# One stage of a four-layer kernel re-ordered by hand: taps of a depthwise convolution moved from VectorE to TensorE, projection and transposes shifted against it

## The chip, the core and the metric

The kernel runs on one core of a Trainium2 chip. TensorE (PE) multiplies matrices and writes to PSUM, VectorE (DVE) and ScalarE (ACT) work elementwise, GpSimd (POOL) copies and multiplies, and SyncE (SP) issues most transfers. The metric is the device time of one execution in microseconds; the median of the runs is given. All data is fp32.

## The reference

The input is x, 8 images of 64 x 64 positions with 192 channels. Four layers each add something to x after a group norm. Layer 0 is a state-space block with convolutions and a feed-forward part, layers 2 and 3 are depthwise 3x3 convolutions. Layer 1 is a scan in four directions; the change lies in its first part:

```
x   = group_norm(x)
xz  = einsum('bhwc,oc->bhwo', x, in_proj_w)         # 192 -> 768 channels
xa, z = split(xz, 2)                                # 384 + 384
u   = silu(depthwise_conv3x3(xa) + conv_b)          # 'SAME', one 3x3 filter a channel
xs  = u, u transposed in space, and both reversed   # the 4 directions
x_dbl = einsum('bkdl,kcd->bkcl', xs, x_proj_weight) # 44 values a position and direction
...                                                 # then the scan over 4096 positions
```

## The kernel before

The program is a sequence of stages: layer 0 (`layer0`), the input stage of layer 1 (`layer1_in`), its scan (`layer1_scan`), and a tail that ends layer 1 and does layers 2 and 3. Each stage reads the last one's result from device memory.

The input stage works on 64 strips: 8 images of 8 strips, a strip being 8 image rows of 64 positions, 512 columns. Channels lie on partitions; the 384 inner channels are three tiles of 128. One strip goes through this:

- `normed` (L690 to L697): load the strip of x1 (`xt`, 384 KB, by SP), and scale and shift it on ACT (`g`, L695, two instructions).
- `project` (L750): for each of three channel tiles two matmuls over the 192 input channels into a PSUM bank "mm"; ACT copies the bank into `xa` (L754), a buffer of ten rows: the strip's eight and one of each neighbour. POOL copies the neighbouring rows between this strip's buffer and the last one's (L758, L759) or clears them at an image's edge (L736, L738).
- `convolve`: for each tile the three taps of the middle column (1, 4, 7 of 0 to 8, with tap = 3 dy + dx + 1) run on PE as matmuls with diagonal matrices (L774) into a bank "cv"; ACT adds the bias and writes `u` (L776); DVE adds the other six taps, each one instruction of 504 elements a partition (L784: 63 of 64 columns, as the outermost has no neighbour).
- `finish` (L797): one Silu on ACT over all three tiles of `u`. It is written into the order after the first tile's bias of the next strip.
- `turn`: SP stores `u` (`ur`, L807). For each of four blocks of 128 positions PE transposes three tiles into a bank "tp" (L813) and multiplies by `w_xp` into a bank "xp" (L816); ACT copies the one into `uT` (L820), DVE the other into `xdt` (L821). SP stores both (`ut` L822, `xd` L823).

All pools of PSUM banks have two buffers. The order of the instructions on PE, DVE, ACT and POOL is that of the program text (`every_engine`, a manual schedule); SP's queue takes its transfers in order too. The text is produced by `together`, which runs the three generators `turn`, `convolve` and `project` in turn, one stretch up to the next `yield` each, while `done` holds back a generator that is too far ahead. So the strip that is turned is the one before the strip that is convolved, and the projection is one to two strips ahead.

Of the kernel before, what the change touches and what calls it, by code (L numbers as in the profile page):

```python
# [10 lines left out]
AF = mybir.ActivationFunctionType  # L11
ALU = mybir.AluOpType
# [3 lines left out]
B, H, W, C = 8, 64, 64, 192  # L16
L = H * W
CP, CT = 96, 2
DIN = 384
DP, DT = 128, 3  # L20
NH, HD, NS = 6, 64, 64
N1, R1, K1 = 16, 12, 4
XC = R1 + 2 * N1
DFF = 768
EPS = 1e-5
NJ = 512
NCH = L // NJ


class Names:  # L30
    n = 0


def mk(pool, shape, tag, **kw):
    Names.n += 1
    return pool.tile(shape, F32, tag=tag, name=f"{tag}_{Names.n}", **kw)


def make_diag(nc, pool, w, nct, ident, tag, plus_one=False):
    P = w.shape[0]  # L40
    dg = mk(pool, [P, nct, 3, P], tag)
    for ct in range(nct):
        for j in range(3):
            s = w[:, ct, 3 * j + 1 : 3 * j + 2]
            if j == 1 and plus_one:
                nc.vector.scalar_tensor_tensor(dg[:, ct, j, :], ident[:P, :P], s, ident[:P, :P], ALU.mult, ALU.add)
            else:
                nc.vector.tensor_scalar(dg[:, ct, j, :], ident[:P, :P], s, None, ALU.mult)
    return dg


# [22 lines left out]
def together(*threads, beside=()):  # L74

    threads = list(threads)
    while threads:
        for t in list(threads) + list(beside):
            if next(t, threads) is threads and t in threads:
                threads.remove(t)  # L80


def every_engine(tc):
    ET = mybir.EngineType
    return tc.manual_schedule(engines={ET.PE, ET.DVE, ET.Activation, ET.Pool})
# [586 lines left out]
def layers123(ctx: ExitStack, tc, a, dr, x1, mv1, out, cst):  # L672
# [30 lines left out]
    xd = [mk(dr, [L, K1, 1 + XC], f"xd{b}") for b in range(B)]  # L703
    yk = [[mk(dr, [L, DIN], f"y{b}_{k}") for k in range(K1)] for b in range(B)]
    layer1_in(tc, a, load, w_in, normed, ur, ut, xd, cst)
    layer1_scan(tc, a, load, ur, ut, xd, yk, cst)
    x2 = [mk(dr, [CP, CT, L], f"x2d{b}") for b in range(B)]
# [4 lines left out]
@with_exitstack  # L712
def layer1_in(ctx: ExitStack, tc, a, load, w_in, normed, ur, ut, xd, cst):

    nc = tc.nc
    ident = cst[0]
    wp = ctx.enter_context(tc.tile_pool(name="wi1", bufs=1))
    cw, cb = load("conv_w", [DP, DT, 9]), load("conv_b", [DP, DT])
    w_xp = load("w_xp", [DP, DT, K1 * XC])
    dg = make_diag(nc, wp, cw, DT, ident, "dg")  # L720
    sb = ctx.enter_context(tc.tile_pool(name="si1", bufs=2))
    psum = ctx.enter_context(tc.tile_pool(name="pi1", bufs=2, space=PSUM))
    xdt = [mk(wp, [128, NJ // 128, K1, 1 + XC], f"xdt{i}") for i in range(2)]
    for t in xdt:
        nc.vector.memset(t, 1.0)
    R = NJ // W
    strips = [(b, r) for b in range(B) for r in range(NCH)]
    rows, us = {}, {}
    done = {"in": 0, "conv": 0, "out": 0}

    def xa_rows(q):

        if q not in rows:
            t = rows[q] = mk(sb, [DP, DT, (R + 2) * W], "xa", bufs=4)
            if strips[q][1] == 0:
                nc.gpsimd.memset(t[:, :, 0:W], 0.0)  # L736
            if strips[q][1] == NCH - 1:
                nc.gpsimd.memset(t[:, :, (R + 1) * W :], 0.0)  # L738
        return rows[q]

    def project():
        _, g = normed(sb, *strips[0])
        for q, (b, r) in enumerate(strips):
            while done["conv"] < q - 2:
                yield
            t = xa_rows(q)
            for o in range(DT):
                ps = mk(psum, [128, NJ], "mm")
                for ct in range(CT):
                    nc.tensor.matmul(  # L750
                        ps, w_in[:, ct, o * 128 : (o + 1) * 128], g[:, ct, :], start=ct == 0, stop=ct == CT - 1
                    )
                yield
                nc.scalar.copy(t[:, o, W : W + NJ], ps)  # L754
            if q + 1 < len(strips):
                _, g = normed(sb, *strips[q + 1])
            if r > 0:
                nc.gpsimd.tensor_copy(t[:, :, 0:W], rows[q - 1][:, :, NJ : NJ + W])  # L758
                nc.gpsimd.tensor_copy(rows[q - 1][:, :, NJ + W :], t[:, :, W : 2 * W])  # L759
            done["in"] = q + 1  # L760
            yield

    def convolve():
        for q, (b, r) in enumerate(strips):
            while done["in"] < q + 1 + (r < NCH - 1) or done["out"] < q - 2:
                yield
            t = rows[q]
            u = us[q] = mk(sb, [DP, DT, NJ], "u", bufs=4)
            uv = u.rearrange("p d (h w) -> p d h w", w=W)
            tv = t.rearrange("p d (h w) -> p d h w", w=W)  # L770
            for o in range(DT):
                ps = mk(psum, [128, NJ], "cv")
                for dy in range(3):
                    nc.tensor.matmul(ps, dg[:, o, dy, :], t[:, o, dy * W : dy * W + NJ], start=dy == 0, stop=dy == 2)  # L774
                yield
                nc.scalar.activation(u[:, o, :], ps, AF.Identity, bias=cb[:, o : o + 1])  # L776
                if o == 0 and q > 0:
                    finish(q - 1)
                yield
                for dy in range(3):  # L780
                    for dx in (-1, 1):
                        w0, w1 = max(0, -dx), W - max(0, dx)
                        tap = 3 * dy + dx + 1
                        nc.vector.scalar_tensor_tensor(  # L784
                            uv[:, o, :, w0:w1],
                            tv[:, o, dy : dy + R, w0 + dx : w1 + dx],
                            cw[:, o, tap : tap + 1],
                            uv[:, o, :, w0:w1],
                            ALU.mult,
                            ALU.add,  # L790
                        )
            yield
        finish(len(strips) - 1)
        yield

    def finish(q):
        nc.scalar.activation(us[q], us[q], AF.Silu)  # L797
        del rows[q]
        done["conv"] = q + 1

    def turn():
        for q, (b, r) in enumerate(strips):
            while done["conv"] < q + 1:
                yield
            u = us.pop(q)
            t0 = r * NJ
            nc.sync.dma_start(ur[b][:, :, t0 : t0 + NJ], u)  # L807
            uT = mk(sb, [128, NJ // 128, DIN], "uT")
            xt = xdt[q % 2]
            for i in range(NJ // 128):  # L810
                ps = mk(psum, [128, NJ], "tp")
                for o in range(DT):
                    nc.tensor.transpose(ps[:, o * 128 : (o + 1) * 128], u[:, o, i * 128 : (i + 1) * 128], ident)  # L813
                px = mk(psum, [128, NJ], "xp")
                for o in range(DT):
                    nc.tensor.matmul(  # L816
                        px[:, 0 : K1 * XC], u[:, o, i * 128 : (i + 1) * 128], w_xp[:, o, :], start=o == 0, stop=o == 2
                    )
                yield
                nc.scalar.copy(uT[:, i, :], ps[:, 0:DIN])  # L820
                nc.vector.tensor_copy(xt[:, i, :, 1:], px[:, 0 : K1 * XC].rearrange("p (k c) -> p k c", k=K1))  # L821
            nc.sync.dma_start(ut[b][t0 : t0 + NJ, :].rearrange("(t q) d -> q t d", q=128), uT)  # L822
            nc.sync.dma_start(xd[b][t0 : t0 + NJ].rearrange("(t q) k c -> q t k c", q=128), xt)  # L823
            done["out"] = q + 1
            yield

    with every_engine(tc):
        together(turn(), convolve(), project())


@with_exitstack
# [621 lines left out]
```

## Time and profile before

| | |
|---|---|
| median of 3 runs | 25105.1 us (25094.24 to 25116.98) |
| profiled execution, span | 25098.0 us (the page gives no time around it) |
| PE busy over the span | 23784.2 us, 95% |
| DVE | 22334.3 us, 89% |
| ACT | 20190.7 us, 80% |
| POOL | 17651.1 us, 70% |
| input stage, first projection to last copy of `xdt` | 5319.4 to 6654.0 us |
| granted TensorE clock, mean | 0.967 |

The shares over the span are averages over stages: the scan alone takes the time from about 6680 to 23000 us. For a change in the input stage its own stretch has to be read. A matmul's busy time in a group holds its latency, and matmuls overlap, so the distance between starts says more of what one costs than the mean of one. An fp32 matmul of the program stands in the trace as two records, a transpose as one. "Idle before, releaser" tells who ended an engine's wait.

### The profile page before, as it was taken

The numbers are of one execution on the slowest core, as the hardware profiler recorded it, in microseconds if no ns is written. First come the engines' busy times: TensorE is split into PE (matmuls) and PEld (weight loads), VectorE is DVE, ScalarE is ACT, GpSimd is POOL, SyncE is SP. The second block draws the span as 40 slices with busy tenths as digits, with TensorE's granted clock in tenths as the row PEclk, the third lists the DMA queues.
The fourth block names the chain that finished last, engine by engine and source line by source line (L and its number), as shares of the span: only waits on it lengthen the run. The fifth ranks groups of instructions, "written<-read, shape, count | busy, mean of one in ns | idle before, by whom it ended". The sixth has DMA issues, their size and how long they took to land.

```text
span 25098.0 us, 445961 instructions
## 1 busy us (share of the span) xinstructions
PE 23784.2 (95%) x156672; PEld 18458.1 (74%) x156672; DVE 22334.3 (89%) x26682; ACT 20190.7 (80%) x40488; POOL 17651.1 (70%) x18332
## 2 busy tenths in 40 slices
PE   8999999988899999999999999999999999998999
PEld 4444444445688888888888888888888888885333
DVE  6777777766799999999999999999999999998887
ACT  4555555544599999999999999999999999997443
POOL 2322322310399999999999999999999999995110
PEclk8888888899999999999999999999999999999999
DMA  1111111123333333333333333333333333335554
GB/s 59 47 43 46 46 47 43 38 70 114 110 100 95 96 101 95 95 103 95 95 101 97 95 99 98 95 97 100 95 95 104 95 95 102 95 95 157 170 175 122
DMA packets 1506272, 2337.12 MB, mean 93 GB/s; under 512 B 249997, under 2 KB 775949, under 8 KB 1504026
## 3 DMA queue, kind: packets, MB, share of 16 engines
q1 hardware_dynamic: 1496858, 2283.42, 31.5%
q8 instruction: 1236, 20.25, 0.3%
q0 software_dynamic: 7168, 25.17, 0.3%
q14 instruction: 1010, 8.27, 0.1%
HBM read 1847.54 MB, written 460.59 MB: 92 GB/s over the span
## 4 chain that ended last, share of the span: by engine, by line
PE 36%; ACT 31%; DVE 13%; POOL 13%; issue 6%; DMA 0%; POOLq 0%; SPq 0%; DVEq 0%; ACTq 0%
ACT dA L1003 13%; POOL hc L1053 11%; ACT sb L987 7%; PE pd L1009 6%; PE yt L942 5%; DVE h L1044 5%; ACT bd L987 4%; PE cv L1282 4%; PE y L592 3%; PE pd L1011 2%; PE mm L901 2%; PE fc L626 2%; PE y L519 1%; PE cv L774 1%; PE tp L564 1%
## 5 line engine op out<-in xcount | busy, mean ns | idle before, releaser
L1053 POOL TENSOR_TENSOR hc<-h,bc 128x512 f32<-128x512 f32 x12288 | 15431.9, 1289 | 475.6 <-DVE h L1044 341.2
L1044 DVE TENSOR_TENSOR_SCAN h<-dA,st,pd 128x512 f32<-128x512 f32 x10752 | 12949.5, 1262 | 530.1 <-PE pd L1009 374.4
L1003 ACT ACTIVATE dA<-dl,A_logs 128x512 f32<-128x512 f32 x12288 | 8817.1, 718 | 47.0 <-DVE h L1044 39.6
L942 PE MATMUL yt<-sq,hc 128*128 128x128 f32 x49152 | 7489.3, 275 | 200.1 <-POOL hc L1053 93.8
L1009 PE MATMUL pd<-bd,dut 128*128 128x128 f32 x49152 | 6581.4, 277 | 254.4 <-DVE h L1044 232.1
L1009 PEld LDWEIGHTS pd<-bd,dut 128*128 128x128 f32 x49152 | 5968.5, 192 | 609.9 <-PE yt L942 342.9
L942 PEld LDWEIGHTS yt<-sq,hc 128*128 128x128 f32 x49152 | 5669.7, 141 | 644.3 <-POOL hc L1053 624.4
L987 ACT ACTIVATE sb<-dut,xt 128x384 f32<-128x384 f32 x8192 | 4779.5, 609 | 1.1 <-DVE dut L928 1.0
L1011 PE MATMUL pd<-sq,sb 128*128 128x128 f32 x24576 | 3739.5, 275 | 8.5 <-DVE h L1044 0.4
L1011 PEld LDWEIGHTS pd<-sq,sb 128*128 128x128 f32 x24576 | 2823.6, 141 | 479.1 <-DVE dl L915 380.8
L987 ACT ACTIVATE bd<-sq,xt 128x128 f32<-128x128 f32 x8192 | 3026.3, 395 | 0.0
L1044 DVE TENSOR_TENSOR_SCAN h<-dA,pd 128x512 f32<-128x512 f32 x1536 | 1770.8, 1204 | 117.0 <-PE pd L1009 67.2
L1143 POOL TENSOR_TENSOR yin<-yin,yin 128x1536 f32<-128x1536 f32 x64 | 233.9, 3655 | 1635.1 <-DMA yin<-y 892.5
L1282 PE MATMUL cv<-x,dgi 96*96 96x512 f32 (+1 forms) x2560 | 1175.0, 595 | 9.3 <-ACT x L1271 9.1
L481 POOL TENSOR_TENSOR xdt<-xb,dtv 128x384 f32<-128x384 f32 x256 | 217.1, 848 | 1186.6 <-ACT xb L475 1186.6
L234 DVE SCALAR_TENSOR_TENSOR x<-xs,cpe_w,x 96x504 f32<-96x504 f32 (+1 forms) x1024 | 886.6, 866 | 31.8 <-ACT x L222 21.7
L784 DVE SCALAR_TENSOR_TENSOR u<-xa,conv_w,u 128x504 f32<-128x504 f32 x1152 | 850.1, 743 | 50.5 <-ACT u L776 12.5
L1282 PEld LDWEIGHTS cv<-x,dgi 96*96 96x96 f32 x2560 | 413.0, 164 | 638.2 <-issue 604.5
L901 PE MATMUL mm<-xs,w_dt 13*128 13x512 f32 x1536 | 863.0, 641 | 1.8 <-DVE dl L915 1.0
L1055 POOL COPY st<-h 128x3 f32<-128x3 f32 x4096 | 825.0, 201 | 0.0
L1303 DVE SCALAR_TENSOR_TENSOR y<-x,wi,y 96x504 f32<-96x504 f32 x1024 | 796.0, 796 | 17.7
L626 PE MATMUL fc<-ff,fc_w 128*96 128x512 f32 x1536 | 791.0, 621 | 2.7 <-DVE xo L629 2.7
(263 smaller groups left out, 26186.7 us busy)
## 6 DMA issues: line engine op xcount, KB each, us to landing
bc<-bcd SPq DMA_DIRECT2D x4096, 256.0 KB
yin<-y SPq DMA_DIRECT2D x256, 768.0 KB
csb<-csd SPq DMA_DIRECT2D x256, 384.0 KB
dut<-ut SPq DMA_DIRECT2D x128, 768.0 KB
y<-ys SPq DMA_DIRECT2D x128, 768.0 KB
dut<-ut SPq DMA_DIRECT2D x256, 384.0 KB
y<-ys SPq DMA_DIRECT2D x256, 384.0 KB
xt<-x1d SPq DMA_DIRECT2D x128, 384.0 KB
```

The lines of the kernel that those rows point to most:

```text
L234: nc.vector.scalar_tensor_tensor(d[:, :, w0:w1], s[:, dy : dy + R, w0 + dx : w1 + dx], w[:, ct, tap : tap + 1], d[:, :, w0:w1], ALU.mult, ...
L626: nc.tensor.matmul(ps, f2w[:, o, ct * CP : (ct + 1) * CP], ff[:, o, :], start=o == 0, stop=o == 5)
L784: nc.vector.scalar_tensor_tensor(uv[:, o, :, w0:w1], tv[:, o, dy : dy + R, w0 + dx : w1 + dx], cw[:, o, tap : tap + 1], uv[:, o, :, w0:w1] ...
L901: nc.tensor.matmul(ps, w_dt[:, k, o * 128 : (o + 1) * 128], made["xs"][0 : 1 + R1, :], start=True, stop=True)
L942: nc.tensor.matmul(yt[:, t * 128 : (t + 1) * 128], src[:, t * 128 : (t + 1) * 128], mat, is_transpose=mat is ident, start=first and t == 0 ...
L987: nc.scalar.activation(v, src, AF.Copy, scale=m["xt"][:, t, 1 + R1 + n : 2 + R1 + n])
L1003: nc.scalar.activation(dA, ready[s]["dl"][:, o, :], AF.Exp, scale=aneg[:, k, o, n : n + 1])
L1009: nc.tensor.matmul(dst, ready[s]["dut"][:, t, cols], brows[g, t], start=True, stop=True)
L1011: nc.tensor.transpose(dst, brows[g, t][:, cols], ident)
L1044: nc.vector.tensor_tensor_scan(h[:, o, rev], decay.pop(j)[:, rev], turned.pop(j)[:, rev], 0.0 if first else st[:, o, n : n + 1], ALU.mult, ...
L1053: nc.gpsimd.tensor_tensor(hc, h[:, o, :], held[g], ALU.mult)
L1282: nc.tensor.matmul(pv[:, :, w0:w1], dgi[:, ct, j, :], sv[:, dy : dy + R, w0 + dx : w1 + dx], start=j == 0, stop=j == len(TAPS) - 1, skip_g ...
```

## The change

Five of the nine taps (the middle column and the middle row: 1, 4, 7, 3, 5) run on PE, four (the corners) on DVE. The generators are gone; the order is written out. The unit is a slot: one channel tile `o` of the strip `c`. In each slot stand, in this order: the five taps of (c, o) on PE; ACT's copy of the projection tile of the slot before; the copies of the blocks turned in the slot before, with the stores after the last block; the Silu of the tile two slots before, now one instruction a tile; bias on ACT and four taps on DVE for (c, o); the projection tile (c+3, o); one turned block of strip c-2 (two in the slot o = 0); and in slot 0 the load and scaling of strip c+4. The loop runs from c = -3 to n+2, and each function does nothing for a strip that does not exist. The ring of `xa` has five buffers instead of four. Which lines of the generators fall away can be seen above; the diff shows what stands in their place.

```diff
--- before.py
+++ after.py
-def make_diag(nc, pool, w, nct, ident, tag, plus_one=False):
+def make_diag(nc, pool, w, nct, ident, tag, taps):
     P = w.shape[0]
-    dg = mk(pool, [P, nct, 3, P], tag)
+    dg = mk(pool, [P, nct, len(taps), P], tag)
...
+        for j, tap in enumerate(taps):
+            nc.vector.tensor_scalar(dg[:, ct, j, :], ident[:P, :P], w[:, ct, tap : tap + 1], None, ALU.mult)
     return dg
-    dg = make_diag(nc, wp, cw, DT, ident, "dg")
+    ON_PE = (1, 4, 7, 3, 5)
+    dg = make_diag(nc, wp, cw, DT, ident, "dg", ON_PE)
...
+    n = len(strips)
+    gs, rows, us, uts = {}, {}, {}, {}
+    banks, turning = {}, []
+
...
+    def reach(tap):
+        dy, dx = tap // 3, tap % 3 - 1
+        return dy, dx, max(0, -dx), W - max(0, dx)
+
+    def normalise(q):
+        if 0 <= q < n:
+            gs[q] = normed(sb, *strips[q])[1]
+
+    def project(q, o):
+        if not 0 <= q < n:
+            return
+        ps = banks["in", q, o] = mk(psum, [128, NJ], "mm")
+        for ct in range(CT):
+            nc.tensor.matmul(
+                ps, w_in[:, ct, o * 128 : (o + 1) * 128], gs[q][:, ct, :], start=ct == 0, stop=ct == CT - 1
+            )
+
+    def projected(q, o):
+        if not 0 <= q < n:
+            return
+        r = strips[q][1]
+        if o == 0:
+            t = rows[q] = mk(sb, [DP, DT, (R + 2) * W], "xa", bufs=5)
+            if r == 0:
                 nc.gpsimd.memset(t[:, :, 0:W], 0.0)
-            if strips[q][1] == NCH - 1:
+            if r == NCH - 1:
                 nc.gpsimd.memset(t[:, :, (R + 1) * W :], 0.0)
-        return rows[q]
-
-    def project():
-        _, g = normed(sb, *strips[0])
-        for q, (b, r) in enumerate(strips):
-            while done["conv"] < q - 2:
-                yield
-            t = xa_rows(q)
+        t = rows[q]
+        nc.scalar.copy(t[:, o, W : W + NJ], banks.pop(("in", q, o)))
+        if o == DT - 1 and r > 0:
+            nc.gpsimd.tensor_copy(t[:, :, 0:W], rows[q - 1][:, :, NJ : NJ + W])
+            nc.gpsimd.tensor_copy(rows[q - 1][:, :, NJ + W :], t[:, :, W : 2 * W])
+
+    def taps_on_pe(q, o):
+        if not 0 <= q < n:
+            return
+        ps = banks["cv", q, o] = mk(psum, [128, NJ], "cv")
+        for i, tap in enumerate(ON_PE):
+            dy, dx, w0, w1 = reach(tap)
+            nc.tensor.matmul(
+                by_rows(ps)[:, :, w0:w1],
+                dg[:, o, i, :],
+                by_rows(rows[q][:, o, :])[:, dy : dy + R, w0 + dx : w1 + dx],
+                start=i == 0,
+                stop=i == len(ON_PE) - 1,
+                skip_group_check=True,
+            )
+
+    def taps_on_dve(q, o):
+        if not 0 <= q < n:
+            return
+        if o == 0:
+            us[q] = mk(sb, [DP, DT, NJ], "u", bufs=4)
+        u = us[q][:, o, :]
+        nc.scalar.activation(u, banks.pop(("cv", q, o)), AF.Identity, bias=cb[:, o : o + 1])
+        for tap in (0, 2, 6, 8):
+            dy, dx, w0, w1 = reach(tap)
+            nc.vector.scalar_tensor_tensor(
+                by_rows(u)[:, :, w0:w1],
+                by_rows(rows[q][:, o, :])[:, dy : dy + R, w0 + dx : w1 + dx],
+                cw[:, o, tap : tap + 1],
+                by_rows(u)[:, :, w0:w1],
+                ALU.mult,
+                ALU.add,
+            )
+        if o == DT - 1:
+            del rows[q]
+
+    def silu(q, o):
+        if not 0 <= q < n:
+            return
+        nc.scalar.activation(us[q][:, o, :], us[q][:, o, :], AF.Silu)
+        if o == DT - 1:
+            b, r = strips[q]
+            nc.sync.dma_start(ur[b][:, :, r * NJ : (r + 1) * NJ], us[q])
+
+    def turn(q, i):
+        if not 0 <= q < n:
+            return
+        u, cols = us[q], slice(i * 128, (i + 1) * 128)
+        ps, px = mk(psum, [128, NJ], "tp"), mk(psum, [128, NJ], "xp")
+        for o in range(DT):
+            nc.tensor.transpose(ps[:, o * 128 : (o + 1) * 128], u[:, o, cols], ident)
+        for o in range(DT):
+            nc.tensor.matmul(px[:, 0 : K1 * XC], u[:, o, cols], w_xp[:, o, :], start=o == 0, stop=o == DT - 1)
+        turning.append((q, i, ps, px))
+
+    def turned():
+        while turning:
+            q, i, ps, px = turning.pop(0)
+            if i == 0:
+                uts[q] = mk(sb, [128, NB, DIN], "uT")
+            nc.scalar.copy(uts[q][:, i, :], ps[:, 0:DIN])
+            nc.vector.tensor_copy(
+                xdt[q % 2][:, i, :, 1:], px[:, 0 : K1 * XC].rearrange("p (k c) -> p k c", k=K1)
+            )
+            if i == NB - 1:
+                b, r = strips[q]
+                t0 = r * NJ
+                nc.sync.dma_start(ut[b][t0 : t0 + NJ, :].rearrange("(t q) d -> q t d", q=128), uts.pop(q))
+                nc.sync.dma_start(xd[b][t0 : t0 + NJ].rearrange("(t q) k c -> q t k c", q=128), xdt[q % 2])
+                del us[q]
+
+    BLOCKS = ((0, 1), (2,), (3,))
+    with every_engine(tc):
+        normalise(0)
+        last = None
+        for c in range(-3, n + 3):
...
             for o in range(DT):
...
-    with every_engine(tc):
-        together(turn(), convolve(), project())
+                taps_on_pe(c, o)
+                if last is not None:
+                    projected(*last)
+                turned()
+                k = DT * c + o - 2
+                silu(*divmod(k, DT))
+                taps_on_dve(c, o)
+                project(c + 3, o)
+                last = c + 3, o
+                for i in BLOCKS[o]:
+                    turn(c - 2, i)
+                if o == 0:
+                    normalise(c + 4)
+        turned()
```

More of the change, by code (lines that the diff above doesn't have):

```diff
@@ L36, in mk @@
     return pool.tile(shape, F32, tag=tag, name=f"{tag}_{Names.n}", **kw)
-def make_diag(nc, pool, w, nct, ident, tag, plus_one=False):
+def make_diag(nc, pool, w, nct, ident, tag, taps):
     P = w.shape[0]
-    dg = mk(pool, [P, nct, 3, P], tag)
+    dg = mk(pool, [P, nct, len(taps), P], tag)
     for ct in range(nct):
[L43 to L48, printed above, removed]
+        for j, tap in enumerate(taps):
+            nc.vector.tensor_scalar(dg[:, ct, j, :], ident[:P, :P], w[:, ct, tap : tap + 1], None, ALU.mult)
     return dg
@@ L719, in layer1_in @@
     w_xp = load("w_xp", [DP, DT, K1 * XC])
-    dg = make_diag(nc, wp, cw, DT, ident, "dg")
+    ON_PE = (1, 4, 7, 3, 5)
+    dg = make_diag(nc, wp, cw, DT, ident, "dg", ON_PE)
     sb = ctx.enter_context(tc.tile_pool(name="si1", bufs=2))
     psum = ctx.enter_context(tc.tile_pool(name="pi1", bufs=2, space=PSUM))
-    xdt = [mk(wp, [128, NJ // 128, K1, 1 + XC], f"xdt{i}") for i in range(2)]
+    NB = NJ // 128
+    xdt = [mk(wp, [128, NB, K1, 1 + XC], f"xdt{i}") for i in range(2)]
     for t in xdt:
@@ L727, in layer1_in, with by_rows @@
     strips = [(b, r) for b in range(B) for r in range(NCH)]
[L728 to L735, printed above, removed]
+    n = len(strips)
+    gs, rows, us, uts = {}, {}, {}, {}
+    banks, turning = {}, []
+    def by_rows(v):
+        return v.rearrange("p (h w) -> p h w", w=W)
+    def reach(tap):
+        dy, dx = tap // 3, tap % 3 - 1
+        return dy, dx, max(0, -dx), W - max(0, dx)
@@ L736, in xa_rows @@
                 nc.gpsimd.memset(t[:, :, 0:W], 0.0)
-            if strips[q][1] == NCH - 1:
+            if r == NCH - 1:
                 nc.gpsimd.memset(t[:, :, (R + 1) * W :], 0.0)
-        return rows[q]
-    def project():
-        _, g = normed(sb, *strips[0])
-        for q, (b, r) in enumerate(strips):
-            while done["conv"] < q - 2:
-                yield
-            t = xa_rows(q)
-            for o in range(DT):
[L748 to L825, printed above, removed]
```

## The prediction

> **What bounds the kernel now.** I read the page's slices first: around 5300 us POOL goes quiet, PE shows 8, 9, 9 and DVE 7, 9, 9, which is the input stage of layer 1. Then the busy time by stretches inside that stage:
>
> ```profile
> core 0: us, PE busy (x) PEld busy (x) DVE busy (x) ACT busy (x) POOL busy (x), PEclk, DMA share, GB/s
> 5560.00:5720.00 160.00, 141.90 (x520) 82.06 (x519) 111.57 (x172) 64.88 (x104) 7.98 (x16) 0.99 0.33 112
> 5720.00:5880.00 160.00, 141.90 (x517) 81.80 (x516) 111.95 (x173) 63.50 (x102) 7.07 (x15) 0.99 0.34 116
> ```
>
> PE is the fullest engine (141.9 of 160 us), DVE is second (112), ACT far behind (64), the DMA engines a third busy. Next the groups of the stretch 5400 to 6520 us, shapes kept apart (x counts instructions; one fp32 matmul of the program stands there as two records, a transpose as one):
>
> ```profile
> L784 DVE SCALAR_TENSOR_TENSOR u<-xa,conv_w,u 128x504 f32<-128x504 f32 x983 | 725.4, 743 | 32.5 <-DVE u L784 0.5
> L774 PE MATMUL cv<-xa,dg 128*128 128x512 f32 x987 | 452.2, 594 | 0.0
> L750 PE MATMUL mm<-g,w_in 96*128 96x512 f32 x656 | 308.6, 592 | 0.0
> L813 PE MATMUL tp<-sq,u 128*128 128x128 f32 x660 | 114.2, 283 | 124.4 <-ACT u L797 124.4
> L797 ACT ACTIVATE u<-u 128x1536 f32<-128x1536 f32 x54 | 80.1, 1483 | 92.8 <-DVE u L784 92.8
> ```
>
> PE's only wait with a name is the first transpose of a strip, for the Silu. The chain that ended last shows the loop behind it, one strip from Silu to the next taps (start, us, what):
>
> ```profile
> 5910.72 1.49 ACT u L797
> 5912.21 0.04 issue
> 5912.25 0.55 PE tp L813 x3
> 5912.80 0.90 PE xp L816 x6
> 5913.69 2.57 PE cv L774 x6
> 5916.27 1.72 PE mm L750 x4
> ...
> 5924.74 0.33 PE tp L813 x3
> 5925.07 0.91 PE xp L816 x6
> 5925.98 0.02 issue
> 5926.00 0.34 DVE xdt L821
> 5926.34 0.66 DVE u L784
> ```
>
> DVE's six taps wait behind the xdt copy, the Silu waits for them, PE waits for the Silu. The starts of the Silu are 20.27 us apart for most strips; ten of the periods read are about 1.4 us longer, and there the records after the wait run at half pace (0.90 us for three transposes instead of 0.55). PE's wait, in the list of waits of 5400 to 6600 us:
>
> ```profile
> PE tp L813 <- ACT u L797: 133.5, 59, 2.3
> ```
>
> So PE idles some 2.3 us a strip. The question is whether the work that the change puts on PE is larger than that.
>
> **The price of PE's work.** A matmul's printed duration (592 ns) holds its latency; in a row of them each takes the distance from start to start, and the chain gives that: 2.58 us for three taps (six records, 0.43 each), 1.72 for a projection tile (four), 0.33 for three transposes, 0.89 for three xp matmuls. A strip has three taps of three tiles, three projection tiles and four turned blocks: 3 x 2.58 + 3 x 1.72 + 4 x (0.33 + 0.89) = 7.74 + 5.16 + 4.88 = 17.78 us. That leaves 20.27 - 17.78 = 2.49 us a strip: the wait of 2.26 and 0.2 of restart.
>
> The two taps that move have 63 of 64 columns of each row, a strided 504-column matmul. The tail of this kernel runs the same form (96 partitions), and its timeline on PE gives the distance:
>
> ```profile
> 24002.91 1.02 PE L1201 MATMUL mm<-zs,w_out 128*96 128x512 f32 x2
> 24003.77 1.01 PE L1282 MATMUL cv<-x,dgi 96*96 96x504 f32 x2
> 24004.62 1.02 PE L1201 MATMUL mm<-zs,w_out 128*96 128x512 f32 x2
> ```
>
> 0.85 us from 24003.77 to 24004.62, against 0.86 for 512 columns: the stride costs nothing, the tap costs two full records.
>
> A rule of the Trainium skill speaks against this price: "TensorE: Matmul & The Clock Gate", section "Back-to-back issue gap", gives N/2.4 + 2.5 ns, 212.5 ns for 504 columns. By it the six added taps would cost an estimated 1.28 us a strip, PE would need 19.06, and the stage would fall by about 108 us. The row shows 850 ns for the same thing in fp32, and the row decides.
>
> **The change, part by part.**
>
> Taps 3 and 5 to PE: 2 x 3 tiles x 0.85 = +5.10 us a strip, all on PE. PE needs 17.78 + 5.10 = 22.88 us a strip, more than the whole period before (20.27). This alone decides the sign, for nothing in the change takes work off PE.
>
> Six taps off DVE: 6 x 0.78 us (743 ns and the gap to the next) = -4.7 us a strip. DVE falls from 15.4 to about 10.7 us of 22.9 and leaves the chain; that gain is worth only PE's idle time.
>
> Turning two strips behind, in written slots: a slot on PE is cv (2.58 + 1.70 = 4.28), one projection tile (1.72), one turned block (1.22; two in slot 0), so 8.44, 7.22 and 7.22 us. Silu of a tile stands two slots after its taps, whose four instructions take 3.1 us, and the turn comes after that: the 2.49 us of waiting go, and the half-pace stretches that follow it (14 us in all). What is late next is nothing but PE itself.
>
> What PE could newly wait for, slot by slot: a "mm" or "cv" bank is written again two slots later and emptied by ACT within one slot. A "tp" or "xp" bank is emptied at the start of the next slot; DVE's xdt copy there stands behind the taps of the last slot, which end about 0.8 us into it (4.28 + 0.69 + 3.1 against 7.22), while the next turn begins 6 us into it. Cover 5 us, price 0. If it were gone, one wait as large as the one removed is the bound: 2.49 us a strip.
>
> Silu in three instead of one: three of 128x512 cost between 1483/3 = 494 ns and 629 ns (the Exp of this shape, SBUF to SBUF, in the scan's first step), so 0 to +0.4 us a strip on ACT, which has 8.7 us of work before and 9.1 after. Hidden by PE; uncovered, 26 us in all.
>
> The xt load is queued on SP behind the ut and xd stores of strip c-3, which wait for that xdt copy: issued about 2 us into slot 0. At the stage's start 4.8 us passed from such an issue (5308.69) to the activation that used it. ACT reaches g about 5 us into the slot, so it may wait up to 2 us; behind it stand the projection copies, needed by PE only in slot 2, 7 us later. Hidden; uncovered at most 2 x 64 = 128 us. The ur store now waits for the Silu of the last tile in slot 1, and the next stores in SP's queue are due a slot later: no one waits. POOL's two halo copies run for strip c+3 while strip c is convolved, so no one waits for them either; their own time (0.4 and 0.7 us) stays.
>
> Nine diagonals become fifteen: 6 x 0.28 = 1.7 us of DVE at the start, beside three strips of projection on PE (15.5 us). One more xa buffer costs no time.
>
> Start and end. The first projection stays at 5319.37, after the group statistics. Its twelve records took 7.39 us instead of 5.16 there: +2.2, as before. In the three strips of projection ahead, ACT has a table load and the exponent of A_logs between its copies (1.6 us): stall 0 to 5, I take 1.5. After the last taps, eight blocks remain to turn, 9.8 us of PE; the first wait for DVE's last taps to let go of the banks (4 us) and the last for the last Silu: 0 to 11 us above PE's work (the upper end by the 2.0 us a block of the old drain, 6646.03 to 6654.03, and one wait), I take 3, nearer to the lower end because a Silu is now a third as long.
>
> **The sum.** Before: from 5319.37 to the last xdt copy's end at 6654.03, 1334.7 us. After: 64 x 22.88 = 1464.3, + 2.2 + 1.5 + 3 = 1471.0. Difference +136 us. Layer 0, the scan and the tail have the same instructions. The profiled execution spans 25098.0 us (the page shows no time around it), 7 below the median of 25105.1 and inside the runs' spread (25094.2 to 25117.0), so I add to the median: 25241 us, +0.54%.
>
> **The rivals.**
>
> The added taps are cheaper than the row (the other side). At one record each (0.43) PE needs 20.33 us, the stage 64 x 20.33 + 6.7 = 1308, -27 us: 25078. Parity lies at (1334.7 - 6.7)/64 = 20.75 us a strip, 0.495 us a tap; faster by 0.2% (50 us, about what a measurement here can tell from none) needs under 0.365. For it: only that 128 partitions were not seen in this form. Against it: 0.85 on 96 partitions, and no matmul of 512 fp32 columns in this trace takes less. 3%.
>
> The written order brings a new wait for PE, in a slot where something above is later than I think. At 0.3 us a slot 64 x 3 x 0.3 = +58 on top: 25299; as large as the old wait, +159: 25400. For it: the engines' order is fixed, and a late xt load blocks all of ACT. Against it: the covers of 5 and 7 us. 12%.
>
> PE without pauses is granted a lower clock. In the tail 0.93 is granted in stretches with 81% PE; at that clock 22.88 becomes 24.6, +110: 25351. Against it: those stretches are the ones with pauses, and the tail's stretch 23300 to 23400 has PE at 99.0 of 100 us with a clock of 1.00. 3%.
>
> **How the numbers follow.** 82% for the forecast, whose own range is 132 (no stall at either end) to 148 (both upper ends), and 11 us of run-to-run spread on each side: 25226 to 25264. The range takes in most of the small-stall case, up to 0.2 us a slot (38 us), and below some 10 us for a drain or start that costs less than before's: 25215 to 25290. Slower holds the forecast, the new wait and the clock, 97%, less 1% for what I have not seen; the cheap tap and that rest give 2% to same and 2% to faster.
>
> **What would show it.** Right: in the changed trace PE at 99% or more of each stretch, clock 1.00, period 22.9 us, the cv group with 1152 records of 512 and 768 of 504 columns, no named wait of PE on ACT, DVE idle for over half. Wrong: a wait of PE on mm, tp or xp by ACT or DVE in the list of waits; g waiting for its load for more than 5 us; the 504-column records closer than 0.42 us; or a period other than the sum of PE's records.

## The result and the profile after

The changed kernel takes 25244.2 us (median of 4 runs, 25239.8 to 25254.1) against 25110.5 us before on the same chip: a ratio of 1.0055, 95% interval 1.0041 to 1.0069. It is slower by 134 us. The profiled execution spans 25241.4 us.

In the changed kernel's lines, the projection is L746, its copy on ACT L761, the taps on PE L772, the bias L787, the taps on DVE L790, the Silu L804, transposes and xp L815 and L817, and the two copies of a turned block L825 (ACT) and L826 (DVE). The busy time by stretches of the input stage, same columns as before:

```profile
core 0: us, PE busy (x) PEld busy (x) DVE busy (x) ACT busy (x) POOL busy (x), PEclk, DMA share, GB/s
5560.00:5720.00 160.00, 160.00 (x547) 89.05 (x547) 70.12 (x112) 58.15 (x105) 10.08 (x14) 1.00 0.30 103
5720.00:5880.00 160.00, 160.00 (x547) 89.05 (x547) 70.12 (x112) 58.15 (x105) 10.08 (x14) 1.00 0.30 103
```

PE no longer pauses: 160.0 of 160 us, at a granted clock of 1.00 (0.99 before). DVE has fallen from 112 to 70. The groups of the stage:

```profile
L790 DVE SCALAR_TENSOR_TENSOR u<-xa,conv_w,u 128x504 f32<-128x504 f32 x768 | 571.3, 744 | 808.1 <-ACT u L787 756.5 <-issue 27.6
L772 PE MATMUL cv<-xa,dg 128*128 128x512 f32 x1152 | 525.7, 592 | 0.0
L746 PE MATMUL mm<-g,w_in 96*128 96x512 f32 x768 | 363.5, 597 | 0.6 <-ACT gn_q L64 0.6
L772 PE MATMUL cv<-xa,dg 128*128 128x504 f32 x768 | 355.9, 586 | 0.0
L804 ACT ACTIVATE u<-u 128x512 f32<-128x512 f32 x192 | 122.7, 639 | 0.7 <-DVE u L790 0.6
```

768 new records of 504 columns stand on PE, and DVE's idle time (808 us) is now due to the bias, which waits for PE's taps. The chain that ended last, over one strip (start, us, what):

```profile
5900.27 4.26 PE cv L772 x10
5904.53 1.72 PE mm L746 x4
5906.25 0.33 PE tp L815 x3
5906.58 0.90 PE xp L817 x6
5907.48 4.26 PE cv L772 x10
5911.74 1.72 PE mm L746 x4
5913.46 0.33 PE tp L815 x3
5913.79 0.90 PE xp L817 x6
5914.69 0.33 PE tp L815 x3
5915.02 0.90 PE xp L817 x6
5915.91 4.26 PE cv L772 x10
```

No ACT and no DVE is left in it. The same place of the pattern returns after 22.86 us (4.26 us pieces at 5907.48 and 5930.34). PE's waits in the whole stage, in the list of waits (us in total, times, longest):

```profile
PE xp L817 <- DVE xdt L826: 1.4, 1, 1.4
PE mm L746 <- ACT gn_q L64: 0.6, 1, 0.6
```

Where the time came from: from the first projection to the end of the last xdt copy the stage took 1334.7 us before (5319.4 to 6654.0) and 1468.5 us after (5326.7 to 6795.2), +133.9. The two profiled executions differ by 143.4 us; the rest is layer 0, which ended 7.1 us later, the scan (4.8 us shorter) and the tail (6.9 longer). Their instructions are the same in both, and these 5 to 7 us lie within the 23 us by which the runs of the kernel before differ among themselves. The difference of the medians, 133.7 us, agrees with the stage's.

### The profile page after: what moved, and what is told of

The parts are those of the page before. It is cut to its first block, busy times and chain, and to the rows that moved or that the text cites. A ratio compares the mean times of both kernels' runs of the same rounds, so it can differ in the third digit from the quotient of the medians.

```text
span 25241.4 us, 447319 instructions
## 1 busy us (share of the span) xinstructions
PE 24084.6 (95%) x157440; PEld 18602.7 (74%) x157440; DVE 22055.2 (87%) x26304; ACT 20193.7 (80%) x40616; POOL 17656.0 (70%) x18332
## 4 chain that ended last, share of the span: by engine, by line
PE 40%; ACT 29%; POOL 13%; DVE 12%; issue 6%; DMA 0%; POOLq 0%; SPq 0%; DVEq 0%; ACTq 0%
ACT dA L1030 12%; POOL hc L1080 11%; PE pd L1036 7%; ACT sb L1014 6%; PE yt L969 6%; DVE h L1071 5%; ACT bd L1014 4%; PE cv L1309 4%; PE cv L772 3%; PE y L588 3%; PE pd L1038 2%; PE mm L928 2%; PE fc L622 2%; PE y L515 1%; PE mm L746 1%
## 5 line engine op out<-in xcount | busy, mean ns | idle before, releaser
L790 DVE SCALAR_TENSOR_TENSOR u<-xa,conv_w,u 128x504 f32<-128x504 f32 x768 | 571.3, 744 | 808.1 <-ACT u L787 756.5
L772 PE MATMUL cv<-xa,dg 128*128 128x512 f32 (+1 forms) x1920 | 850.3, 590 | 0.0
```

The lines of the kernel that those rows point to most:

```text
L772: nc.tensor.matmul(by_rows(ps)[:, :, w0:w1], dg[:, o, i, :], by_rows(rows[q][:, o, :])[:, dy : dy + R, w0 + dx : w1 + dx], start=i == 0, s ...
```

## The experiments

All ratios are against the kernel before, on the same chip. "Period" is the distance of the same instruction from one strip to the next in the middle of the stage; "stage" runs from the first projection to the end of the last xdt copy in the profiled execution. The time of the kernel before in the table is that of the chip on which e1 to e4 ran; on the chips of the changed kernel, e5 and e6 it was 25110.5, 25114.8 and 25108.0 us.

| kernel | taps on PE, by tile | order | period, us | stage, us | time, us | ratio, 95% interval |
|---|---|---|---|---|---|---|
| before | 3, 3, 3 | generators | 20.27 | 1334.7 | 25108.9 | |
| changed | 5, 5, 5 | slots | 22.86 | 1468.5 | 25244.2 | 1.0055, 1.0041 to 1.0069 |
| e1 | 3, 3, 3 | slots | 17.79 | 1150.7 | 24925.7 | 0.9929, 0.9914 to 0.9944 |
| e2 | 5, 5, 5 | generators | 23.51 | 1521.9 | 25296.9 | 1.0076, 1.0061 to 1.0091 |
| e3 | 4, 4, 4 | slots | 20.32 | 1307.3 | 25086.4 | 0.9991, 0.9982 to 1.0001 |
| e4 | 2, 3, 3 | slots | 16.93 | 1103.3 | 24878.3 | 0.9908, 0.9894 to 0.9923 |
| e5 | 2, 3, 2, xdt copy on ACT | slots | 16.07 | 1043.9 | 24826.6 | 0.9885, 0.9868 to 0.9901 |
| e6 | 3, 3, 3 | generators, turning two behind | 17.79 | 1156.3 | 24924.3 | 0.9926, 0.9909 to 0.9942 |

### The order without the taps

```diff
-    ON_PE = (1, 4, 7, 3, 5)
+    ON_PE = (1, 4, 7)
...
-        for tap in (0, 2, 6, 8):
+        for tap in (0, 2, 3, 5, 6, 8):
```

> The written order alone: taps 3 and 5 go back to VectorE, so three taps run on TensorE and six on VectorE as before; all else is the changed kernel. Theory (TensorE's summed records set the period, the order removes its waits): 22.86 - 6 x 0.85 = 17.8 us a strip on TensorE, VectorE 15.3 and ScalarE 9.1 under it, no wait of TensorE for the Silu; the stage takes 64 x 17.8 + 5.5 = 1145 us against 1334.7 before, so about 190 us less than the kernel before: 24920 us. Rival (VectorE, now ending 2.4 us into the next slot, or ScalarE's order, holds TensorE up in place of the Silu): a period between 18.5 and 20.3 us, 24960 to 25105 us, with waits of TensorE on xp or u in the list.

Measured: 24925.7 us and a period of 17.79, the theory's numbers. A stretch of it:

```profile
5720.00:5880.00 160.00, 160.00 (x596) 93.86 (x595) 129.45 (x198) 74.81 (x135) 12.24 (x17) 1.00 0.38 132
```

PE is full here too, with less work in it per strip. The slots alone take 183 us off the kernel before (25108.9 to 24925.7), and the two taps a tile then put 318.5 on (to 25244.2). The stage alone says the same: 184 us less, then 318 more.

### The taps without the order

```diff
+    ON_PE = (1, 4, 7, 3, 5)
...
-                for dy in range(3):
-                    nc.tensor.matmul(ps, dg[:, o, dy, :], t[:, o, dy * W : dy * W + NJ], start=dy == 0, stop=dy == 2)
+                for i, tap in enumerate(ON_PE):
...
+                    nc.tensor.matmul(
+                        pv[:, :, w0:w1],
+                        dg[:, o, i, :],
+                        tv[:, o, dy : dy + R, w0 + dx : w1 + dx],
+                        start=i == 0,
+                        stop=i == len(ON_PE) - 1,
+                        skip_group_check=True,
+                    )
...
-                for dy in range(3):
+                for dy in (0, 2):
                     for dx in (-1, 1):
```

> The taps alone: the kernel before with its three generators, five taps on TensorE and four on VectorE. Theory (sum of records): in the old order TensorE had 4.3 us of taps and projection beside 6.5 us of last taps and Silu, hence its wait of 2.3; with five taps it has 6.0 us beside 5.0, so the wait goes without any re-ordering and the period is again 22.9 us; with the old start and end about 25240 to 25270 us, within 0.1% of the changed kernel. Rival (the wait was removed by the order, and stays in the old one): 22.9 + 2.5 = 25.4 us a strip, about 25400 us.

Measured: 25296.9 us, between the two. Most of the old wait is gone without any re-ordering, as the theory had it: PE's wait for the Silu fell from 133.5 us to this, over the same 5400 to 6600 us:

```profile
PE tp L820 <- ACT u L804: 22.0, 51, 0.4
```

But the theory had left something out, and the chain shows it:

```profile
5901.07 4.28 PE cv L774 x10
5905.35 0.02 issue
5905.38 0.02 ACT u L783
5905.40 0.56 issue
5905.96 1.48 ACT u L804
5907.44 0.04 issue
5907.49 0.55 PE tp L820 x3
```

The Silu (L804) does not wait for DVE's last taps any more. It stands on ACT behind the bias (L783) of the next strip's first tile, and that bias waits for the five taps on PE, which take 4.28 us now. After them PE has only one projection tile (1.72 us) to do, while ACT has bias and Silu; 0.65 us of PE's time are lost in each strip (period 23.51 against 22.86: the wait of 0.4 and the restart, 0.55 us for three transposes instead of 0.33). Times 64 that is 42 us; the rest of the 53 us between this kernel and the changed one lies at the stage's start and end (17 us above the sum of periods here, 5.5 there).

So the order is worth 183 us at three taps and 53 at five.

### Four taps

```diff
-    ON_PE = (1, 4, 7, 3, 5)
+    ON_PE = (1, 4, 7, 3)
...
-        for tap in (0, 2, 6, 8):
+        for tap in (0, 2, 5, 6, 8):
```

> One tap (5) of the five goes back to VectorE in the changed kernel: four on TensorE, five on VectorE. Theory (a tap costs TensorE two full records, 0.85 us a tile): 22.86 - 3 x 0.85 = 20.3 us a strip, 163 us less than the changed kernel, 25080 us, about 25 us under the kernel before. Rival (the strided tap is cheaper in the row than its share of the group, or the stage is not set by TensorE): less than 100 us below the changed kernel.

Measured: 25086.4 us, period 20.32, 158 us under the changed kernel. From three to four to five taps the period goes 17.79, 20.32, 22.86: 0.845 us for each strided tap of a tile, twice. With four taps the added work has used up what the slots gain: the interval of the ratio holds 1.

### Fewer taps: where DVE begins to matter

On top of e1, where `ON_PE` is (1, 4, 7); `on_pe` is `taken(o)`:

```diff
+    def taken(o):
+        return (1, 7) if o == 0 else ON_PE
...
         for i, tap in enumerate(ON_PE):
+            if tap not in on_pe:
+                continue
...
-        for tap in (0, 2, 3, 5, 6, 8):
+        for tap in range(9):
+            if tap in taken(o):
+                continue
```

> The written order with taps 1 and 7 on TensorE for the first channel tile of a strip and 1, 4, 7 for the other two; VectorE does the rest (19 instructions of taps a strip). Theory: TensorE needs 17.8 - 0.86 = 16.9 us, VectorE 19 x 0.775 + 1.35 = 16.1, so TensorE still sets the period: 16.9 us, 55 us under the kernel with three taps everywhere, about 24865 us. Rival (with 95% of a period VectorE has no room left and its late copies hold TensorE up): 17.3 us or more, no gain over three taps.

Measured: 24878.3 us, period 16.93 as in the theory; the gain on e1 is 47 us instead of 55. DVE is at 142 of 160 us, and PE is still full in the middle:

```profile
5560.00:5720.00 160.00, 160.00 (x611) 95.65 (x610) 142.15 (x218) 78.68 (x144) 12.53 (x17) 1.00 0.43 141
```

The missing 8 us are at the two ends, in the waits of PE over the whole stage:

```profile
PE xp L825 <- DVE xdt L834: 13.9, 7, 3.3
```

There the slots lack the turning or the projection and are shorter than DVE's taps in them; DVE falls behind, and PE waits for it to empty a bank. In e1 the same wait sums to 6.8 us, in the changed kernel to 1.4.

And on top of that:

```diff
-        return (1, 7) if o == 0 else ON_PE
+        return (1, 4, 7) if o == 1 else (1, 7)
...
-            nc.vector.tensor_copy(
+            nc.scalar.copy(
                 xdt[q % 2][:, i, :, 1:], px[:, 0 : K1 * XC].rearrange("p (k c) -> p k c", k=K1)
```

> As the run with two, three, three taps, but two taps (1 and 7) also for the third tile, and the copy of xp into xdt moved from VectorE to ScalarE. Theory (whichever engine has the largest sum sets the period): TensorE 16.93 - 0.86 = 16.07 us a strip, VectorE 20 taps x 0.775 = 15.5, ScalarE 8.3 + 4 x 0.4 = 9.9; TensorE still sets it, 55 us less, about 24825 us. Rival (VectorE at 96% and ScalarE's longer in-order queue make TensorE wait): a period of 16.5 us or more, a gain under 30 us, and waits of TensorE or VectorE on ScalarE in the list.

Measured: 24826.6 us, period 16.07, again PE's sum. DVE is at 147.4 and ACT at 95.3 of 160 us. This is the fastest of the kernels tried, 1.15% under the kernel before, with two taps a strip fewer on PE than that had. The run changes two things at once. By the theory's prices DVE would need an estimated 20 x 0.775 + 1.35 = 16.9 us a strip if it kept the copy, more than PE's 16.07; a kernel with the tap moved and the copy left on DVE was not run.

### One condition of the old order

```diff
-            while done["conv"] < q + 1:
+            while done["conv"] < min(q + 2, len(strips)):
                 yield
             u = us.pop(q)
```

> The kernel before with one condition changed: a strip is turned when two further strips are through their Silu in the program's order, so the strip turned is two behind the one convolved. Generators, three taps on TensorE and the one large Silu stay. Theory (the old wait was only this: the first transpose directly behind the Silu): TensorE's sum of 17.8 us a strip is the period again, with at most 0.7 us of small waits, as ScalarE's Silu still stands ahead of its copies of the projection: 17.8 to 18.5 us, 24930 to 24980 us, so that the shift alone brings at least 130 of the 183 us that the written order brought at three taps. Rival (the slots and the Silu by tile matter as much): 18.9 us or more, over 25000 us, with waits of TensorE on ScalarE's copies or VectorE's.

Measured: 24924.3 us and a period of 17.79, the same as the slots with three taps (24925.7). The rival fell: the slots, the projection three strips ahead and the Silu by tile together add nothing that can be measured, at three taps, to turning one strip later. The Silu still waits for DVE here, as before (starts of two strips, columns start, us, what, and idle before it):

```profile
5750.73 1.48 ACT L797 ACTIVATE u<-u 128x1536 f32<-128x1536 f32 x1 [1.72 <-DVE u L784]
5768.52 1.48 ACT L797 ACTIVATE u<-u 128x1536 f32<-128x1536 f32 x1 [1.72 <-DVE u L784]
```

but no transpose stands behind it any more, and PE is full:

```profile
5720.00:5880.00 160.00, 160.00 (x596) 93.52 (x595) 128.62 (x198) 72.85 (x117) 8.54 (x18) 1.00 0.39 132
```

## Why the prediction was right, point by point

**The price of the added taps.** +5.10 us a strip was predicted from the distance of one such matmul in the tail, on 96 partitions. Measured on 128: 6 x 0.845 = 5.07. This step carried the sign, and the rival of the cheaper tap, which had only the unseen 128 partitions for it, falls with e1 and e3. The estimate from the Trainium skill's page "TensorE: Matmul & The Clock Gate", section "Back-to-back issue gap" (212.5 ns for 504 columns) does not hold for these fp32 matmuls: from one period to the next the two records of such a tap take 845 ns.

**What the removed wait is worth.** PE's sum of 17.78 us for three taps, taken from the chain of the kernel before, is the period of e1 and e6, 17.79. The waits that the change removes are 20.27 - 17.79 = 2.48 us a strip, less than the 5.07 that it adds. Over 64 strips the difference of 2.59 makes 166 us, not the 134 measured: beyond its 64 periods the kernel before lost 37 us (14 of them in the ten longer strips, and 6.6 in one last wait of PE for the Silu), the changed kernel 5.5. That the written order would bring no new wait in the middle of the stage is right: no wait of PE is listed there, and the 1.4 us come in the last strips. The clock was 1.00, so the third rival falls too.

**The sum.** Predicted 64 x 22.88 + 6.7 = 1471.0 us, measured 64 x 22.86 + 5.5 = 1468.5. The forecast of 25241 us is 3 us from the median. Part of this closeness is luck. At the start 2.2 us were predicted for records at half pace and 1.5 for PE waiting for ACT behind the table load. PE waited for nothing there: its 36 records took 18.95 us to the first tap instead of 15.5, because the granted clock was 0.52 from 5326 to 5334 us, so the half pace alone made up the 3.5. At the end 2.0 us were lost instead of 3.

**Where single steps were off.** The xt load was placed behind the stores of its slot, with up to 2 us of waiting for the activation. No such wait exists. The timeline of the changed kernel (ACT and SP, one period):

```profile
5912.37 1.51 ACT L691 ACTIVATE g<-xt,nbb,scb 96x512 f32<-96x512 f32 x2
5913.90 0.56 SPq L688 DMA_DIRECT2D xt<-x1d  x1
5935.22 1.51 ACT L691 ACTIVATE g<-xt,nbb,scb 96x512 f32<-96x512 f32 x2
```

SP's transfers are not bound to the slot, as SP is not among the engines whose order `every_engine` fixes. With two buffers of `xt`, the load that goes out at 5913.90 takes the buffer that the activation before it let go of at 5913.88. It is two strips ahead of that activation, and its data is used two periods, some 44 us, after its issue. The slot of the program text says nothing of this; the prediction should have read it from SP's own order. A Silu of one tile takes 639 ns, a little over the upper end of 629; three of them cost ACT 0.43 us a strip more than the one, hidden as said. For DVE and the drain the prediction named the right instruction (the xdt copy behind the last taps), and e4 shows what it costs when DVE's cover shrinks: 13.9 us at the ends.

**What the prediction did not ask.** It priced the removed wait and the added taps in one sum. Apart, they are -183 and +318.5 us, and the first needs one changed condition instead of a new order.

## What to carry to other kernels

On an engine that is nearly full, add up its instructions by the distance between their starts, once for the work and once for the period: the difference is all that a re-ordering can bring in the steady part, and work moved onto that engine counts against it at full price. Look for the one place where the full engine stands directly behind a chain of the others (here the first transpose behind the Silu), and put a strip between the two before anything is rewritten. Then share the work by the sums per strip: here six more taps of a strip on TensorE cost 318 us, and two fewer, with one small copy shifted to ScalarE, gave 99.

## What the runs showed of the hardware

In the kernel before, ten of some sixty strips were 1.4 us longer, with PE's records at half pace right after its wait of 2.3 us. The wait itself was the same in a strip that was not hit and in the next one, which was:

```profile
5870.37 0.55 PE L813 MATMUL tp<-sq,u 128*128 128x128 f32 x3 [2.26 <-ACT u L797]
5890.64 0.90 PE L813 MATMUL tp<-sq,u 128*128 128x128 f32 x3 [2.26 <-ACT u L797]
```

With waits of 0.4 us (e2) or none the granted clock was 1.00 in every stretch read from the middle of the stage. The Trainium skill, "TensorE: Matmul & The Clock Gate", section "Part 1: The HAM clock gate (the "warmup" mystery)", puts the fall to half clock at an idle window of about 3.4 us; here pauses of 2.3 us, once in 20 us, were enough for some strips.

Which strips these are, the record of the granted clock in the same trace tells. In this stage the clock changes only at points that lie whole steps of 3.41 us apart, and from 5400 to 6600 us each stretch at half clock lasts one such step (5890.02 to 5893.43 us at the second line above). A period of 20.27 us is 0.21 us short of six steps, so the wait begins 0.21 us earlier in its step from strip to strip. Of the 59 waits from 5400 to 6600 us, the nine that began at most 1.77 us behind a point were all followed by half clock, and none of the 50 that began 1.84 us or more behind one was. The 1.4 us lost then put the next wait 1.2 us later in its step, and six or seven strips pass before it happens again. As these waits are all 2.26 us long, what tells the strips that were hit from the others is where the wait falls in the step.
